# Reordering the first gathers, powers and weight loads of each layer in a four-layer perceiver kernel, with a shared part placed amid the causal tail

## The chip, the cores and the metric

One NeuronCore of a Trainium2 chip runs the whole kernel. The metric is device time in microseconds (us) of one execution; the median of three executions before the change is 2838.52 us (2836.55 to 2840.55).

The engines are named as the profile names them: PE (matrix products), PEld (weight loads of PE), DVE (vectors), ACT (activations), POOL (general purpose; it also issues the indirect gathers) and SP (issues most plain DMAs). Each engine runs its own instructions in one order and waits on semaphores for the others.

## The reference

The input x has 16 batches of 64 tokens with 256 features (1024 tokens); ctx has 16 x 1024 rows of 192. Four layers follow, each of three residual steps on the normalised x:

```python
# L0: cross attention to ctx, causal attention, mixture of 8 experts (top 2) with a shared expert
x = x + L0_xattn(layernorm(x), ctx, ctx); x = x + L0_attn(layernorm(x)); x = x + L0_ffn(layernorm(x))
# L1: cross attention (16 heads), convolution + running pooled attention + gelu layer, 8 experts top 2
x = x + L1_xattn(layernorm(x), ctx); x = x + L1_attn(layernorm(x)); x = x + L1_ffn(layernorm(x))
# L2: cross attention (8 heads of 64), complex linear recurrence, 8 experts top 2 with capacity
x = x + L2_xattn(layernorm(x), ctx); x = x + L2_attn(layernorm(x)); x = x + L2_ffn(layernorm(x))
# L3: cross attention (8 heads of 64), selective state space, dense layers with +1/-1 weights
x = x + L3_xattn(layernorm(x), ctx); x = x + L3_attn(layernorm(x)); x = x + L3_ffn(layernorm(x))
```

A mixture layer picks two experts per token by softmaxed logits, applies each expert's two- or three-matrix network, and adds the results weighted by the gates.

## The kernel before

All of x stays on chip as eight tiles `xs[:, i, :]` of 128 tokens by 256 features. The stages run one after another and overlap at their borders: `L0_first` (cross attention, causal attention and routing interleaved), `L0_ffn`, `L1_xattn`, `L1_attn`, `L1_ffn`, `L2_xattn_attn`, `L2_ffn` and `L3`.

**Who sets the order.** The kernel is written in a framework that places the instructions of each engine by a planner, in the order of the program and by when their inputs are ready. Inside `manual_schedule(engines=...)` the named engines keep the order of the program among the instructions written there; instructions written elsewhere may still be put between them. In most stages PE alone is fixed; at the start of `L1_xattn` (L1014) PE and DVE are. Python generators cut a job into pieces, and a stage calls `next` on them at chosen places so that one job's products fill another's waits.

**Mixture layers.** Routing (`route_setup` L1130 onwards, `route`, `block_experts` L1313) takes the logits, the two best experts, ranks the tokens of each expert, and sorts them into blocks of 128 tokens that have one expert each. `block_experts` yields after `rows` (which rows of the weight matrices a block gathers) and then makes `tokens` (which tokens it takes). A block gathers the weights `wa` and `wb` by `rows` and its tokens' features `hb` from the DRAM table `hs` by `tokens`, all on POOL through `gather_rows` (L1386), three buffers deep; it transposes hb on PE (L179), runs its products (`gu` or `ph`, then `po`), and writes `yb` to the DRAM table `ys` on ACT's queue (`block_out`, L1408 to L1410). `L0_ffn` has 23 blocks at most, the last 5 under a condition; `L1_ffn` 15. Padding reads a zero row of `hs` or `ys`, written by `zeros` (L1143); `route_setup` is called three times and writes the zero row of `hs` each time (L1140).

The next stage carries a tile (`carry`, L1388): two gathers `back` (or `p`) from `ys` by `route_at`, each added to xs by DVE (L1395). Then comes the normalisation: statistics on DVE (L154, L156, L158), a power on POOL (L160), and `o` on DVE (L458 in `heads64`, L890 in `L1_xattn`), which PE transposes.

**End of L0_first.** `attn.go()` is a round: each causal tile under way, and the routing of the group of two tiles that is at its turn, takes one step. After the last cross attention tile a loop calls `go` until nothing is left, and after each round one piece of the shared expert: `shared_part(k)` yields three times after a pair of gate and up products (`gu`, eight PE instructions) and twice after a down product (`po`, six). Chunk k is 256 tokens (tiles 2k and 2k+1). Chunks 0 and 1 go there; chunks 2 and 3 are written in `L0_ffn`, after both halves of `block_experts`, without a fixed order.

**Start of L1_xattn.** `keys_values(b)` gives four pieces (keys, values, keys, values) of PE work on a batch's context; their results leave the PSUM buffers `misc` through DVE or ACT. `queries(i)` carries and normalises tile i in its first step, transposes in its second, and makes qs with a copy by DMA in its third.

**L1_attn and L1_ffn.** The string `turns` (L1710) spells which of six generators steps next: parts 0 to 3 and the routing of tiles 0 to 3 and of tiles 4 to 7 (digits 2 and 5).

**L2_xattn_attn.** `recurrence()` (L1739) writes its set-up (powers on POOL L1749 and L1752, some 20 small DVE steps for angles from L1765 on, a sine on ACT) and returns the object whose `go` does a piece of the state recurrence. `heads64` does the cross attention and calls `breathe` (here `go`) at its filling places, first after tile 0 has been normalised.

**L3.** `first` multiplies two small matrices on PE (`large<-w_dt,w_xT`, 32 instructions). `weights` (L1988) issues the loads of L3a_in, L3a_bc and L3a_out, and through `fetch_L3_ffn` (L1910) those of the dense layers, on SP; some of them go as early as their room is free.

Of the kernel before, what the change touches and what calls it, by code (L numbers as in the profile page):

```python
# [42 lines left out]
class Net:  # L43
# [242 lines left out]
    def L0_first(self):  # L286
# [19 lines left out]
        with self.tc.manual_schedule(engines={mybir.EngineType.PE}):  # L306
# [90 lines left out]
            shared = chain(*(self.shared_part(k) for k in range(2)))  # L397
# [269 lines left out]
    def causal_attention(self, wqkv, wproj):  # L667
# [4 lines left out]
        s = SimpleNamespace(ready=0, next=0, work=[], behind=[])  # L672
# [138 lines left out]
        def routing(g):  # L811
# [41 lines left out]
    def L1_xattn(self):  # L853
# [160 lines left out]
        with self.tc.manual_schedule(engines={mybir.EngineType.PE, mybir.EngineType.DVE}):  # L1014
            biases()
            for piece, turn in zip(keys_values(0), (None, *[queries(0)] * 3)):
                piece()
                if turn is not None:
                    next(turn)
        with self.tc.manual_schedule(engines={mybir.EngineType.PE}):  # L1020
            held, work = None, {}
            one, two = queries(1), queries(2)
            ahead = (one,), (one, two), (one, two), (two,)
            steps = [(b, g) for b in range(B) for g in range(4)]
            for k in range(len(steps) + 4):
# [15 lines left out]
                if k < len(steps):  # L1041
                    if more:
                        more.pop(0)()
                    if not b:
                        for turn in ahead[g]:
                            next(turn)
                    elif b % 2 == 0 and g < 3 and b // 2 + 2 < NT:
                        if not g:
                            ahead = queries(b // 2 + 2)
                        next(ahead)  # L1050
# [76 lines left out]
    def route_setup(self, k):  # L1127
# [86 lines left out]
    def L0_block(self, j, own):  # L1214
        w = self.lp.tile([128, 4 * 704], F32, tag="wa" + own, bufs=1 if own else 3, name="wa")
        self.gather_rows(w, self.a["L0f_w13"], self.rows[j][:, j : j + 1])
        w2 = self.lp.tile([128, 6 * D], F32, tag="wb" + own, bufs=1 if own else 3, name="wb")
        self.gather_rows(w2, self.a["L0f_w2r"], self.rows[j][:, j : j + 1])
        return w.rearrange("p (c f) -> p c f", c=2), w2.rearrange("p (m f) -> p m f", f=D)
# [22 lines left out]
    def L0_ffn(self):  # L1242
        nc = self.nc
        self.blocks(self.routed, L0_BLOCKS)
        self.tag, self.tag_bufs = "gu", 4
        self.hid_tag, self.hid_bufs = "hid1", 3
        for k in range(2, NC):
            for _ in self.shared_part(k):
# [3 lines left out]
        def block(j, own=""):  # L1252
            w13, w2 = self.L0_block(j, own)
            dT = self.block_tokens(j, own)
# [50 lines left out]

    def blocks(self, r, n_blocks):


        rest = self.block_experts(r, n_blocks)
        next(rest)  # L1310
        next(rest, None)
# [87 lines left out]
    def block_tokens(self, j, own=""):  # L1399

        hb = self.lp.tile([128, D], F32, tag="hb" + own, bufs=1 if own else 3, name="hb")
        self.gather_rows(hb, self.hs, self.tokens[:, j : j + 1])
# [9 lines left out]
    def L1_block(self, j, own=""):  # L1412
        w = self.lp.tile([128, 2 * 1024 + 8], F32, tag="wa" + own, bufs=1 if own else 3, name="wa")
        self.gather_rows(w, self.a["L1f_W1b"], self.rows[j][:, j : j + 1])
        w2 = self.lp.tile([128, 8 * D], F32, tag="wb" + own, bufs=1 if own else 3, name="wb")
        self.gather_rows(w2, self.a["L1f_W2r"], self.rows[j][:, j : j + 1])
        return (
            w[:, : 2 * 1024].rearrange("p (c f) -> p c f", f=1024), w[:, 2 * 1024 :],
# [3 lines left out]
    def L1_ffn(self):  # L1422
        nc = self.nc
        def block(j, own=""):
            w1, b1, w2 = self.L1_block(j, own)
            dT = self.block_tokens(j, own)
# [106 lines left out]
    def L1_attn(self):  # L1533
# [970 lines left out]
```

## Time and profile before

| | |
|---|---|
| median of three executions | 2838.52 us |
| profiled execution, its own time | 2838.53 us |
| span of its trace | 2836.7 us |
| busy PE / PEld / DVE / ACT / POOL | 2603.1 / 1889.9 / 1399.4 / 1003.4 / 311.8 us |
| mean granted clock of PE | 0.963 |

The stretches about the places that the change touches, from the trace, with PE's busy time, the granted PE clock (1.00 is full) and the DMA engines' mean busy share:

| stretch, us from the start | what runs | PE busy, us | clock | DMA share |
|---|---|---|---|---|
| 60 to 255 | L0_first | 167.83 of 195 | 0.89 | 0.31 |
| 255 to 286 | causal tail, routing, first gathers of L0_ffn | 24.73 of 31 | 0.83 | 0.52 |
| 1083 to 1112 | end of L1_attn, first gathers of L1_ffn | 17.57 of 29 | 0.57 | 0.38 |
| 1220 to 1236 | start of L2_xattn_attn | 3.02 of 16 | 0.61 | 0.09 |
| 1930 to 1950 | start of L3 | 15.08 of 20 | 1.00 | 0.46 |

How to read it: the times are those of one profiled execution. A timeline line gives the start, the duration, the engine, the source line, the operation and its tiles (out<-in); the brackets at its end give the time the engine idled just before and what ended it. An instruction stands under the line of the helper that issued it: L69 is every product through `mm`, L62 and L64 are copies out of PSUM, L179 a transpose, L131 a weight load.

### The profile page before, as it was taken

To read this page: it belongs to the slowest core of one execution; us is meant where nothing else is said; L and a number is where in the kernel's file an instruction comes from. 1 tells how busy PE (TensorE), PEld (TensorE's weight loads), DVE (VectorE), ACT (ScalarE), POOL (GpSimd) and SP (SyncE) were. 2 spreads that over 40 slices of the span, in tenths; PEclk is the share of its full clock that TensorE was granted. 3 is DMA by queue.
4 is the path that set the end of the run, shared out by engine and by line. 5 is a ranking of instruction groups with operands and counts; after the bars stand their busy time and mean duration, and the time that the engine had idled before them with its cause. 6 is when DMAs were issued, how large, how long until landed. Compare 5 with 4: busy or idle time off the path is not lost.

```text
span 2836.7 us, 44734 instructions
## 1 busy us (share of the span) xinstructions
PE 2603.1 (92%) x18116; PEld 1889.9 (67%) x18116; DVE 1399.4 (49%) x2825; ACT 1003.4 (35%) x2114; POOL 311.8 (11%) x429
## 2 busy tenths in 40 slices
PE   7888998999999898979999999698999998998999
PEld 3556895666666686856666666695666665666777
DVE  3556225666666643233434342423344756658692
ACT  1323223555555441222222222122234545455330
POOL 1111333000000112310001000201001000000000
PEclk9988999999999997989999999799999999999999
DMA  8512872100100114801111111463112213121110
GB/s 244 174 49 77 339 271 65 31 27 28 38 27 23 42 38 176 305 25 47 59 58 55 45 49 59 181 239 108 51 49 91 86 49 97 56 76 30 61 45 8
DMA packets 79228, 253.71 MB, mean 89 GB/s; under 512 B 15151, under 2 KB 26954, under 8 KB 69290
## 3 DMA queue, kind: packets, MB, share of 16 engines
q1 hardware_dynamic: 59562, 165.01, 18.0%
q0 software_dynamic: 13312, 80.28, 7.9%
q10 hardware_dynamic: 6144, 5.51, 0.6%
q8 instruction: 145, 2.38, 0.3%
q14 instruction: 65, 0.53, 0.1%
HBM read 233.80 MB, written 14.82 MB: 88 GB/s over the span
## 4 chain that ended last, share of the span: by engine, by line
PE 38%; DVE 9%; ACT 3%; issue 2%; DMA 2%; POOL 1%; SPq 1%; DVEq 0%; ACTq 0%; POOLq 0%
PE sc L505 9%; PE ps_h L69 5%; PE misc L541 4%; PE halves L69 3%; PE misc L69 3%; PE ps_t L519 3%; PE halves L541 3%; PE misc L536 2%; PE gu L69 2%; DVE x L2104 2%; PE halves L2128 2%; PE halves L536 1%; DVE nmx L223 1%; DVE x L2100 1%; DMA rep<-dus 1%
## 5 line engine op out<-in xcount | busy, mean ns | idle before, releaser
L223 DVE TENSOR_REDUCE nmx<-sc 128x1 f32<-128x1024 f32 x264 | 311.7, 1218 | 228.4 <-PE sc L505 144.8
L225 ACT ACTIVATE p<-sc,nmx 128x1024 f32<-128x1024 f32 x264 | 294.2, 1115 | 313.5 <-DVE nmx L223 313.3
L505 PE MATMUL sc<-ctxT,qp 128*128 128x512 f32 (+1 forms) x1024 | 357.5, 603 | 0.0
L505 PEld LDWEIGHTS sc<-ctxT,qp 128*128 128x128 f32 (+1 forms) x1024 | 139.4, 190 | 155.4 <-issue 152.3
L519 PE MATMUL ps_t<-ident,p 128*128 128x128 f32 x1024 | 140.2, 279 | 40.2 <-ACT pT L522 17.3
L2094 ACT ACTIVATE da<-rep,al 128x252 f32<-128x252 f32 x256 | 115.9, 500 | 134.4 <-DVE x L2104 124.2
L519 PEld LDWEIGHTS ps_t<-ident,p 128*128 128x128 f32 x1024 | 115.3, 142 | 65.2 <-ACT pT L522 21.0
L2104 DVE TENSOR_TENSOR_SCAN x<-da,x 128x512 f32<-128x512 f32 x128 | 152.7, 1218 | 2.7 <-ACT da L2094 1.9
L235 PE MATMUL misc<-ident,p 128*128 128x128 f32 x1024 | 137.1, 279 | 7.2 <-ACT p L225 6.8
L522 ACT COPY pT<-ps_t 128x512 f32<-128x512 f32 x166 | 94.0, 587 | 122.0 <-PE ps_t L519 116.1
L235 PEld LDWEIGHTS misc<-ident,p 128*128 128x128 f32 x1024 | 110.1, 141 | 32.7 <-ACT p L225 15.4
L160 POOL TENSOR_TENSOR ln_rs<-ln_ve,nhalf 128x1 f32<-128x1 f32 x80 | 44.9, 567 | 692.8 <-DVE ln_ve L158 611.0
L541 PE MATMUL halves<-pT,ctx 128*128 128x256 f32 x512 | 119.3, 386 | 0.0
L541 PE MATMUL misc<-pT,ctx 128*128 128x256 f32 x512 | 119.1, 386 | 0.0
L237 ACT COPY pT<-misc 128x512 f32<-128x512 f32 x128 | 75.0, 586 | 108.6 <-PE misc L235 108.1
L69 PE MATMUL ps_h<-r,w 128*128 128x256 f32 x512 | 113.4, 381 | 0.0
L2100 DVE TENSOR_TENSOR x<-rep,bc_rep 128x512 f32<-128x512 f32 x128 | 84.7, 687 | 57.9 <-PE halves L2128 55.2
L239 DVE COPY pT<-misc 128x512 f32<-128x512 f32 x128 | 88.3, 690 | 39.7 <-PE misc L235 28.6
L69 PEld LDWEIGHTS ps_h<-r,w 128*128 128x128 f32 x512 | 96.6, 190 | 15.9 <-issue 2.5
L541 PEld LDWEIGHTS halves<-pT,ctx 128*128 128x128 f32 x512 | 94.8, 190 | 17.3 <-issue 5.6
L541 PEld LDWEIGHTS misc<-pT,ctx 128*128 128x128 f32 x512 | 94.6, 190 | 17.1 <-issue 5.5
L69 PE MATMUL po<-wb,hid 128*128 128x256 f32 x440 | 100.3, 379 | 0.0
(500 smaller groups left out, 4504.3 us busy)
## 6 DMA issues: line engine op xcount, KB each, us to landing
ctx<-in_ctx SPq DMA_DIRECT2D x48, 768.0 KB, 4.4
ctxT<-in_ctxT SPq DMA_DIRECT2D x48, 512.0 KB, 3.3
w<-in_L2f_W SPq DMA_DIRECT2D x24, 1024.0 KB, 8.3
rep<-dus SPq DMA_DIRECT2D x256, 64.0 KB, 1.9
ctxT<-in_ctxT SPq DMA_DIRECT2D x16, 768.0 KB, 15.5
ctxT<-in_ctxT SPq DMA_DIRECT2D x96, 128.0 KB, 3.5
ys<-yb ACTq DMA_DIRECT2D x40, 128.0 KB, 5.7
bc_rep<-bcs SPq DMA_DIRECT2D x32, 128.0 KB, 3.0
```

Of the source, the lines that this page charges most:

```text
L69: self.nc.tensor.matmul(out, lhsT, rhs, start=n == 0, stop=n == len(pairs) - 1)
L223: self.nc.vector.tensor_reduce(nmx, sc, AX.X, ALU.max, negate=True)
L225: self.nc.scalar.activation(p, sc, AF.Exp, bias=nmx, accum_out=sums)
L235: self.nc.tensor.transpose(ps[:, u, :], p[:, at : at + 128], self.ident)
L239: self.nc.vector.tensor_copy(pT[:, 0:4, :], ps)
L505: nc.tensor.matmul(sc[u][:, bass.ts(kh, 512)], qp[n][par][rows, h : h + 2, :].rearrange("p h q -> p (h q)"), ctx[0][rows, at], start=n == ...
L519: nc.tensor.transpose(ps[:, t, :], p[:, at : at + 128], self.ident)
L522: nc.scalar.copy(to, ps)
L541: nc.tensor.matmul(o, ck[:, t, :128], pT[:, t].rearrange("p u q -> p (u q)"), start=t == 0, stop=t == NK - 1)
L2094: nc.scalar.activation(da[:, g, :, 1:], now[j][:, 0, :].rearrange("p (b s) -> p b s", s=S)[:, :, 1:], AF.Exp, scale=al[:, col : col + 1],)
L2100: nc.vector.tensor_tensor(h, now[j][:, 1:2, :].to_broadcast([128, 2, CHUNK]), bc[:, 0, states, :], ALU.mult)
L2104: nc.vector.tensor_tensor_scan(flat, da.rearrange("p g b s -> p (g b s)"), flat, 0.0, ALU.mult, ALU.add)
```

## The change

There are six edits.

1. `zeros` copies from the last row of the causal mask tile, which is zero throughout, in 4 packets of 256 bytes in place of 256 packets of 4; the zero row of `hs` is written by the first routing only.
2. Chunk 2 of the shared expert joins the loop at the end of `L0_first`. A part begins only when the features of its tiles are there (`turned`, set in the routing generator). In `L0_ffn`, PE is now fixed: first half of `block_experts`, two pieces of chunk 3, second half, the rest of chunk 3.
3. At the start of `L1_xattn` POOL is fixed too, and six pieces of keys and values (four of batch 0, two of batch 1) alternate with three steps of tile 0's queries.
4. The second routing of `L1_attn` yields after two of its four tiles' logits, and `turns` gives it one step earlier.
5. The first block of `L0_ffn` and of `L1_ffn` gathers wa, hb, wb in that order, fixed on POOL (before: wa, wb, hb); the other blocks as before.
6. At layer 2 `recurrence()` is made at the first call of `breathe`; at layer 3 six one-column copies of the updated tile 0 go into the rooms of the weights before their loads are issued.

```diff
             del self.ctxT[2:], self.ctx[2:]
-            shared = chain(*(self.shared_part(k) for k in range(2)))
+
+            def parts():
+                for k in range(3):
+                    while attn.turned <= k:
+                        yield
+                    yield from self.shared_part(k)
+
+            shared = parts()
             while attn.go():
                 next(shared, None)
...
+            s.turned = g + 1
             ps = self.misc([128, 2, E])
...
-        with self.tc.manual_schedule(engines={mybir.EngineType.PE, mybir.EngineType.DVE}):
+        with self.tc.manual_schedule(
+            engines={mybir.EngineType.PE, mybir.EngineType.DVE, mybir.EngineType.Pool}
+        ):
             biases()
-            for piece, turn in zip(keys_values(0), (None, *[queries(0)] * 3)):
-                piece()
-                if turn is not None:
+            turn = queries(0)
+            ahead = keys_values(0) + keys_values(1)
+            for n in range(6):
+                ahead.pop(0)()
+                if n in (1, 3, 4):
                     next(turn)
...
-                        more = keys_values(b + 1) if b + 1 < B else None
-                    if not k:
-                        more.pop(0)()
+                        more = ahead if not b else keys_values(b + 1) if b + 1 < B else None
...
-        self.zeros(self.hs[:1])
+        if self.routed is None:
+            self.zeros(self.hs[:1])
...
     def zeros(self, row):
         self.nc.sync.dma_start(
-            row.rearrange("p (d o) -> p d o", o=1), self.lanes[:1, :1].unsqueeze(1).to_broadcast([1, D, 1])
+            row.rearrange("p (r d) -> p r d", d=S), self.causal[S - 1 : S].unsqueeze(1).to_broadcast([1, D // S, S])
         )
...
+    def gathered(self, j, own, first, second):
+
+        got = []
+        with self.tc.manual_schedule(engines={mybir.EngineType.Pool}) if not j else nullcontext():
+            order = ("wa", "hb", "wb") if not j else ("wa", "wb", "hb")
+            for name in order:
...
     def L0_ffn(self):
         nc = self.nc
-        self.blocks(self.routed, L0_BLOCKS)
         self.tag, self.tag_bufs = "gu", 4
         self.hid_tag, self.hid_bufs = "hid1", 3
-        for k in range(2, NC):
-            for _ in self.shared_part(k):
+        with self.tc.manual_schedule(engines={mybir.EngineType.PE}):
+            experts, part = self.block_experts(self.routed, L0_BLOCKS), self.shared_part(NC - 1)
+            next(experts)
+            for _ in range(2):
+                next(part)
+            next(experts, None)
+            for _ in part:
                 pass
...
         def routing(first):
             ps = self.misc([128, 4, E])
             for t in range(4):
+                if first and t == 2:
+                    yield
...
-        turns = "0010130134013004314101340301301403101341041134031434234323424242455555"
+        turns = "00101301340130043141013403013014031013410411340314342343234242452455555"
...
         with self.tc.manual_schedule(engines={mybir.EngineType.PE}):
-            lru = self.recurrence()
-            self.heads64(breathe=lru.go, finished=lru.more)
+            made = []
+
+            def lru():
+                if not made:
+                    made.append(self.recurrence())
+                return made[0]
+
+            self.heads64(breathe=lambda place: lru().go(place), finished=lambda i: lru().more(i))
...
         def weights():
-            for n, to in zip(("in", "bc", "out"), (w[0], w[2], w[3])):
+            rooms = w[0], w[2], w[3], self.spent[0], w[4], self.spent[1]
+            for to in rooms:
+                nc.vector.tensor_copy(to[:, 0, :1], self.xs[:, 0, :1])
+            for n, to in zip(("in", "bc", "out"), rooms):
                 nc.sync.dma_start(to, self.a[f"L3a_{n}"])
             yield
-            self.ffn = self.fetch_L3_ffn((self.spent[0], w[4], self.spent[1]))
+            self.ffn = self.fetch_L3_ffn(rooms[3:])
```

More of the change, by code (lines that the diff above doesn't have):

```diff
@@ L671, in causal_attention @@
         nc = self.nc
-        s = SimpleNamespace(ready=0, next=0, work=[], behind=[])
+        s = SimpleNamespace(ready=0, next=0, turned=0, work=[], behind=[])
         sb = self.sb
@@ L1022, in L1_xattn @@
             one, two = queries(1), queries(2)
-            ahead = (one,), (one, two), (one, two), (two,)
+            turns = (one,), (one, two), (one, two), (two,)
             steps = [(b, g) for b in range(B) for g in range(4)]
@@ L1044, in L1_xattn @@
                     if not b:
-                        for turn in ahead[g]:
+                        for turn in turns[g]:
                             next(turn)
@@ L1048, in L1_xattn @@
                         if not g:
-                            ahead = queries(b // 2 + 2)
-                        next(ahead)
+                            turn = queries(b // 2 + 2)
+                        next(turn)
                 if held is not None:
@@ L1212, in route, with L0_block @@
             self.over_experts(g, ALU.add, "", r.gates[x][:, tiles])
[L1214 to L1219, printed above, removed]
+    def gathered(self, j, own, first, second):
[3 more added lines that the diff above has]
+            for name in order:
+                bufs = 1 if own else 3
+                if name == "hb":
+                    hb = self.lp.tile([128, D], F32, tag="hb" + own, bufs=bufs, name="hb")
+                    self.gather_rows(hb, self.hs, self.tokens[:, j : j + 1])
+                else:
+                    src, n = first if name == "wa" else second
+                    w = self.lp.tile([128, n], F32, tag=name + own, bufs=bufs, name=name)
+                    self.gather_rows(w, self.a[src], self.rows[j][:, j : j + 1])
+                    got.append(w)
+        return hb, *got
+    def L0_block(self, j, own=""):
+        hb, w, w2 = self.gathered(j, own, ("L0f_w13", 4 * 704), ("L0f_w2r", 6 * D))
+        return hb, w.rearrange("p (c f) -> p c f", c=2), w2.rearrange("p (m f) -> p m f", f=D)
     def shared_part(self, k):
@@ L1252, in block @@
         def block(j, own=""):
-            w13, w2 = self.L0_block(j, own)
-            dT = self.block_tokens(j, own)
+            hb, w13, w2 = self.L0_block(j, own)
+            dT = self.block_tokens(hb)
             hid = self.lp.tile([128, 6, 128], F32, tag="hid1", bufs=3, name="hid1")
@@ L1304, in ranks @@
         return rank
[L1306 to L1311, printed above, removed]
     def block_experts(self, r, n_blocks, later=False):
@@ L1397, in carry, with block_tokens @@
             )
-    def block_tokens(self, j, own=""):
-        hb = self.lp.tile([128, D], F32, tag="hb" + own, bufs=1 if own else 3, name="hb")
-        self.gather_rows(hb, self.hs, self.tokens[:, j : j + 1])
+    def block_tokens(self, hb):
         dT = self.lp.tile([128, 2, 128], F32, tag="dT", bufs=2, name="dT")
@@ L1412, in L1_block @@
     def L1_block(self, j, own=""):
[L1413 to L1416, printed above, removed]
+        hb, w, w2 = self.gathered(j, own, ("L1f_W1b", 2 * 1024 + 8), ("L1f_W2r", 8 * D))
         return (
-            w[:, : 2 * 1024].rearrange("p (c f) -> p c f", f=1024), w[:, 2 * 1024 :],
+            hb, w[:, : 2 * 1024].rearrange("p (c f) -> p c f", f=1024), w[:, 2 * 1024 :],
             w2.rearrange("p (m f) -> p m f", f=D),
@@ L1424, in block @@
         def block(j, own=""):
-            w1, b1, w2 = self.L1_block(j, own)
-            dT = self.block_tokens(j, own)
+            hb, w1, b1, w2 = self.L1_block(j, own)
+            dT = self.block_tokens(hb)
             hid = self.lp.tile([128, 8, 128], F32, tag="hid", bufs=2, name="hid")
@@ L1732, in L2_xattn_attn @@
         with self.tc.manual_schedule(engines={mybir.EngineType.PE}):
-            lru = self.recurrence()
-            self.heads64(breathe=lru.go, finished=lru.more)
+            made = []
[4 more added lines that the diff above has]
+            self.heads64(breathe=lambda place: lru().go(place), finished=lambda i: lru().more(i))
             self.start_pack(self.at)
-            while lru.go():
+            while lru().go():
                 pass
```

## The prediction

> **What bounds the kernel now.** I read the page's first two blocks first. Its busy times, and the slices of PE and of its granted clock:
>
> ```profile
> PE 2603.1 (92%) x18116; PEld 1889.9 (67%) x18116; DVE 1399.4 (49%) x2825; ACT 1003.4 (35%) x2114; POOL 311.8 (11%) x429
> ...
> PE   7888998999999898979999999698999998998999
> ...
> PEclk9988999999999997989999999799999999999999
> ```
>
> PE is busy for 92% of 2836.7 us, so the time is PE's work plus PE's waits. The dips stand where a layer begins, and there the clock falls too. Next I read PE's timeline at each start that the diff touches: end of layer 0's causal attention, layer 1's cross attention, layer 1's experts, layer 2 and layer 3. Columns are start, duration, engine, line, operation, and in brackets the idle time with what ended it.
>
> ```profile
> 255.77 1.03 PE L69 MATMUL misc<-w,yT 128*128 128x256 f32 x4
> ...
> 260.78 4.13 PE L69 MATMUL gu<-hT,w 128*128 128x256 f32 x18
> ...
> 268.29 1.94 PE L69 MATMUL misc<-s_col,s_who 128*64 128x128 f32 x8 [2.83 <-DVE s_col L1186]
> 270.17 0.60 PE L69 MATMUL misc<-route_seen,ones 128*128 128x8 f32 x2
> 273.01 4.64 PE L69 MATMUL gu<-hT,w 128*128 128x256 f32 x10 [2.25 <-DVE hid L1234]
> 277.58 0.57 PE L69 MATMUL misc<-at_block,route_table 64*128 64x23 f32 x2
> 278.08 2.87 PE L69 MATMUL misc<-w,hid 128*128 128x256 f32 x12
> ...
> 284.67 0.38 PE L179 MATMUL misc<-ident,hb 128*128 128x128 f32 x2
> ```
>
> ```profile
> 454.77 0.66 PE L179 MATMUL misc<-ident,o 128*128 128x128 f32 x2 [4.68 <-DVE o L890]
> ...
> 467.07 1.13 PE L69 MATMUL sc<-kT,qs 32*128 32x512 f32 x4 [2.21 <-DMA qs<-qs]
> ```
>
> ```profile
> 1110.41 0.69 PE L179 MATMUL misc<-ident,hb 128*128 128x128 f32 x2 [2.10 <-DMA hb<-hs,tokens]
> ```
>
> ```profile
> 1232.95 0.66 PE L179 MATMUL misc<-ident,o 128*128 128x128 f32 x2 [12.47 <-DVE ln_mv L156]
> ```
>
> ```profile
> 1931.26 13.90 PE L69 MATMUL large<-w_dt,w_xT 128*128 128x512 f32 x32
> 1949.39 0.44 PE L179 MATMUL halves<-ident,o 128*128 128x128 f32 x2 [4.24 <-DVE o L458]
> 1950.39 3.65 PE L69 MATMUL large<-hT,w 128*128 128x128 f32 x16 [0.56 <-issue]
> ```
>
> In the first fence shared-expert products (gu) fill nearly every wait of layer 0's tail, so the chain from projection 255.77 to block counts 270.17 costs PE little. The others show true waits of 4.68, 2.21, 2.10, 12.47 and 4.24 us. Only these, and the time that a late chain adds, can change.
>
> **Part 1: the zero row.** Before, 256 packets of 4 bytes, three times; after, 4 of 256 bytes, once. Such a packet takes 9 ns in the trace: 256 x 9 / 16 engines = 0.14 us of DMA. The issue takes SP 0.59 us against 0.33 for a plain load. Only the first issue (18.91 us) is near busy DMAs. I take **-0.2** (0 to -1).
>
> **Part 2: the shared part in the causal tail.** Parts 0 and 1 already go one piece per round. A part is three gu pieces of 1.99 us and two po pieces of 1.47: 8.9 us. After the change part 2's pieces go in rounds 11 to 15, in PE's fixed order ahead of the last tile's weighing and projection; the planner had put only 1.13 us (gu, 254.80) there. So the projection comes 8.9 - 1.13 = 7.8 us later; I take 7.7. Projection to end of counts is a chain of small DVE steps, 15.0 us now. It ends at 270.77 + 7.7 = 278.5. The 4.13 us of gu that hid inside it (260.78) are gone from there, so PE idles in it. Part 3 is then fixed behind the counts: 24 gu and 12 po instructions, 8.9 us at full clock; at the half clock, by the rows 273.01 (4.64/10 = 0.464 each) and 278.08 (2.87/12 = 0.239 each), 11.1 + 2.9 = 14.0. I take the middle, 11.5, with 0.57 for the tokens: PE reaches block 0 at 290.6 instead of 284.67. Its tokens agree: two pieces (16 gu at a mean of 0.36, 5.7) and the product 0.57 end at 284.8; from there to the gathered rows took 283.48 - 278.15 = 5.3 us, so 290.1. Weights: the gather issued at 274.40 landed at 281.01, so 7.7 later 288.7, hidden by part 3. That the second weights now gather behind hb costs 0.95 us of POOL issue, needed only after 44 products (5.15 us). Term **+5.9**. Bounds: 0, if the chain waits for DVE anyway and the pieces lie in that wait; above, 14.0 for part 3 (293.1, +8.4) and block 0's 5.15 at half clock too: +13.6.
>
> The granted clock in the profile is 0.50 from 267.72 to 277.96, after PE's 2.83 us wait, and 0.97 from 264 to 268. The Trainium skill, TensorE: Matmul & The Clock Gate, section Part 1: The HAM clock gate, says that the array falls to half rate after an idle window of about 3.4 us and comes back after one sustained busy window; it speaks against moving work out of waits, as here. By it only part 3's first 3.4 us would be slow, 1.7 us more than 8.9, and the term +5.0; the row's 10.24 us is three such windows, so I stay with the rows.
>
> **Part 3: layer 1's cross attention.** PE waits 4.68 us for o of tile 1 (L890). Its adds end at 450.9, its variance at 452.16, but POOL issues two gathers for other tiles (451.19, 452.44) before the power at 453.54. POOL's fixed order puts the power ahead of them: up to 1.4 us. DVE's order holds kT's eviction (454.55) behind that o, and the next keys' products need the bank: so the wait can't be filled altogether. One key or value piece (2.9 us) of batch 1 goes ahead of scores, in place of a later one; it can cover the 2.21 us wait for qs, whose copy took 4.2 us beside a context load. I take 1.4 + about 0.3: **-1.7** (bounds -5, from 4.68 + 2.21 less their 2.9 us of filler missing later, and +1, a POOL gather of 0.95 queued behind a power that waits).
>
> **Part 4: layer 1's routing and first block.** Four tiles' logits take PE 1086.28 to 1091.57. Two go a turn earlier, so the chain starts about 1.4 us sooner. Behind it, hb is gathered before the second weights: issued 1104.14 before, landed 1110.37. Together hb lands near 1106.5 and the 2.10 us wait goes; PE's gate work before it ends 1.4 sooner, 1107. But DMA runs full from 1102 to 1128, and block 1's rows (landed 1117.68, used 1119.95) become late next: about 2.2 us of slack. I take **-1.2** (0 to -3).
>
> **Part 5: layer 2's start.** ys lands at 1223.72; POOL gathers at once, then runs a power of the recurrence's set-up (1224.70, 0.89), gather 2 (1226.87) and another power (1227.91, 0.59). DVE stands at L1792 behind that power until 1228.5, so the carry's add, whose rows landed at 1226.50, runs at 1229.99 only. Made after the first two tiles, the set-up can't stand there: the add runs at 1226.6, 3.4 sooner; PE at 1229.5. Up to 3.85 if the gather's landing alone decides. About 21 DVE steps of 0.15 to 0.25 us and a table load of 1.28 come later, beside score products of 7.25 us. I take **-3.3** (-1 to -3.85).
>
> **Part 6: layer 3's weights.** About 3.3 MB of loads are issued on SP before the last block's rows are written:
>
> ```profile
> 1930.28 0.33 SPq L1990 DMA_DIRECT2D w<-in_L3a_in  x1
> ...
> 1931.60 0.58 SPq L1910 DMA_DIRECT2D w<-in_L3f_k  x1
> ```
>
> The write issued at 1931.64 by ACT landed 8.25 us later, with a DMA share of 0.95 and 0.82 in the two stretches of 4 us from 1932; the same write at layer 2's start took 2.68 (1221.04 to 1223.72). The four gathers went at 1941.09 and after. Six one-column copies of DVE, which read the updated tile 0, hold the loads back. The gathers then go some 5.6 to 6.3 us sooner. PE has w_dt x w_xT until 1945.16, so it gains the idle 4.24 and, the clock (granted 0.50 from 1950.49 to 1953.91) no longer falling, most of 3.65 - 1.95 (the same 16 products at 1982.03) = 1.7: **-5.9** (-3, half of the write's delay being other than these loads, to -7.5). The copies cost 6 x 0.15 us of DVE; SP has no issue between 1931.60 and 1974.54, so nothing queues behind the held loads, which then run while DMA is nearly idle (1948 to 1972). Without this cover, their 2.7 MB would take 8 us of the context loads. The weights are first read near 2060.
>
> **Sum:** -0.2 + 5.9 - 1.7 - 1.2 - 3.3 - 5.9 = -6.4. The profiled execution took 2838.53 us (span 2836.7 and 1.8 around it), the median 2838.52, so it carries over: **2832.1 us**. About 0.2% (5.7 us) is what a measurement can tell from no change: below 2832.8 counts as faster, above 2844.2 as slower.
>
> **Rivals.**
> *The tail decides (slower).* Part 2 at its full price: the chain pushed 7.7 and the clock half over part 3 and block 0, +13.6. For it: 10.24 us at half clock after an idle time of only 2.83; against it: gu pieces warm the array. It overtakes the five gains (12.3) from +12.3. With them whole the time is 2839.8; with layers 2 and 3 at their small ends (-1, -3) it is 2845.
> *Larger gain.* The pieces lie in the tail's DVE waits (part 2 at +1), and both waits of layer 1's attention go (-4): -0.2 + 1 - 4 - 2 - 3.5 - 6.5 = -15.2, 2823. For it: PE waited in that stretch often enough for 3.6 us of filler; against it: kT's bank.
> *It doesn't do what it says.* The write of ys is slow for another reason than these loads, and layer 2's add waits for its landing: -0.2 + 5.9 - 1 - 0.5 - 1 - 3 = +0.2, 2838.7. For it: the last write always ends after a block of big loads; against it: 2.68 us at layer 2.
>
> **Chances.** Forecast 0.42 (own range 2828 to 2836; 0.25 of it below 2832.8), larger gain 0.22, not as said 0.20 (all within), tail 0.16 (0.13 above 2844.2, 0.03 within). Faster 0.47, same 0.40, slower 0.13. The range runs from 2822 to 2845: the larger gain and the tail's dear end just in.
>
> **What would show it.** The counts' product near 278 and block 0's rows near 290; the wait before o of tile 1 nearer 3 than 5; hb's wait gone at layer 1's experts; layer 2's first product near 1229 less the shift; the last write in 3 us at layer 3 and no idle time before its first transposes. It would be wrong if the counts come at their old distance, or if the first gathers at layer 3 aren't sooner.

## The result and the profile after

The changed kernel took 2848.01 us (median of 9 runs, 2844.14 to 2852.86) against 2838.52 (2834.1 to 2844.97): a ratio of 1.0033, 95% interval 1.0022 to 1.0045. It is 9.5 us slower, where the forecast was 2832.1 and faster. The profiled execution has a span of 2846.2 us, 9.5 more than before.

From the page of the changed kernel:

```profile
PE 2608.7 (92%) x18116; PEld 1892.2 (66%) x18116; DVE 1402.5 (49%) x2831; ACT 1003.2 (35%) x2114; POOL 310.1 (11%) x429
```

PE does the same 18116 products; its busy time has grown by 5.6 us (the same products, part of them at a lower clock) and its waits by 3.9.

A good way to find where two executions of one program part is to match each product with its twin and to follow how far the later one lags. The lag (after minus before, in us) is -0.4 at 40, -9.5 at 56, -10.9 at 200 to 240, -2.8 at the block counts, -4.1 at block 0 of layer 0, +1.4 from block 2 on; +2.4 in layer 1's attention, +8.6 at the end of its experts, +9.9 in layer 2; +10.1 at the end of layer 2, +5.0 at the start of layer 3, +9.4 at the end. So there is an early gain that the forecast hadn't, a loss of 12.3 us between 240 and 300, the expected gain at layer 3, and several small losses. Every lag in this document is taken against one profile of the kernel before; how far that profile itself is from other executions is told below.

PE's timeline of the changed kernel at the places shown before, first the end of the causal tail:

```profile
267.36 0.60 PE L69 MATMUL misc<-route_seen,ones 128*128 128x8 f32 x2
269.53 6.04 PE L69 MATMUL gu<-hT,w 128*128 128x256 f32 x16 [1.58 <-DVE past L1352]
275.50 0.40 PE L69 MATMUL misc<-at_block,route_table 64*128 64x23 f32 x2
...
280.58 0.38 PE L179 MATMUL misc<-ident,hb 128*128 128x128 f32 x2
...
293.08 0.44 PE L179 MATMUL misc<-ident,hb 128*128 128x128 f32 x2 [3.71 <-DMA hb<-hs,tokens]
```

Counts 8.1 us and block 0 6.8 us later against the stretch before them (lag -10.9), near the 7.7 and 5.9 worked out; most of the two pieces of chunk 3 ahead of the tokens runs at half clock (6.04 us for 16 products; the granted clock is 0.50 from 257.22 to 274.28). New is the last line: block 1 waits 3.71 us for its rows.

Then layer 1's cross attention, layer 1's experts, layer 2, layer 3 on PE, and layer 3's loads on SP:

```profile
458.03 0.44 PE L179 MATMUL misc<-ident,o 128*128 128x128 f32 x2 [2.00 <-DVE ln_ve L158]
...
468.27 3.26 PE L948 MATMUL misc<-w,ctxT 128*128 128x256 f32 x8 [4.28 <-DVE kT L939]
```

```profile
1115.53 0.69 PE L179 MATMUL misc<-ident,hb 128*128 128x128 f32 x2
...
1126.76 0.44 PE L179 MATMUL misc<-ident,hb 128*128 128x128 f32 x2 [0.84 <-DMA hb<-hs,tokens]
```

```profile
1242.44 0.66 PE L179 MATMUL misc<-ident,o 128*128 128x128 f32 x2 [13.34 <-DVE ang_y L1792]
```

```profile
1955.08 0.38 PE L179 MATMUL halves<-ident,o 128*128 128x128 f32 x2
1956.02 2.02 PE L69 MATMUL large<-hT,w 128*128 128x128 f32 x16 [0.56 <-ACT w L2011]
```

```profile
1953.69 0.33 SPq L2018 DMA_DIRECT2D w<-in_L3a_in  x1
```

In layer 1 one wait has been exchanged for another twice (4.68 + 2.21 for 2.00 + 4.28; 2.10 for 0.84 one block later). Layer 2 waits 0.9 us longer than before. Layer 3 is as forecast: no wait, and the 16 products in 2.02 in place of 3.65.

The early gain stands in PE's waits for the second context load. Before:

```profile
45.94 1.94 PE L340 MATMUL sc<-ctxT,qp 96*64 96x512 f32 x2 [3.81 <-DMA ctxT<-in_ctxT]
49.68 6.82 PE L340 MATMUL sc<-ctxT,qp 96*64 96x512 f32 x14 [1.79 <-DMA ctxT<-in_ctxT]
```

After:

```profile
43.38 3.65 PE L340 MATMUL sc<-ctxT,qp 96*64 96x512 f32 x14 [0.78 <-DMA ctxT<-in_ctxT]
```

The first wait is gone, the second is 0.78 us, and the 14 products take 3.65 us at full clock (granted 1.00 from 18.28 to 72.90; before 0.50 from 45.86 to 56.10). A wait of 1.47 us for the same tensor comes later, at 56.67. In before, the packets of 4 KB of that load, issued at 34.63, took up to 5.97 us each, in the 7 us after 256 packets of 4 bytes had been written, most of them from 32 to 33.

### The profile page after: what moved, and what is told of

Same layout as the page of the kernel before. It is cut to its first block, busy times and chain, and to the rows that moved or that the text cites. A ratio compares the mean times of both kernels' runs of the same rounds, so it can differ in the third digit from the quotient of the medians.

```text
span 2846.2 us, 44754 instructions
## 1 busy us (share of the span) xinstructions
PE 2608.7 (92%) x18116; PEld 1892.2 (66%) x18116; DVE 1402.5 (49%) x2831; ACT 1003.2 (35%) x2114; POOL 310.1 (11%) x429
## 4 chain that ended last, share of the span: by engine, by line
PE 40%; DVE 9%; ACT 3%; issue 2%; DMA 2%; POOL 1%; SPq 1%; ACTq 0%; DVEq 0%; POOLq 0%
PE sc L512 9%; PE ps_h L69 5%; PE misc L548 4%; PE halves L69 3%; PE misc L69 3%; PE ps_t L526 3%; PE halves L548 2%; PE gu L69 2%; PE misc L543 2%; PE halves L2156 2%; DVE x L2132 2%; DVE nmx L223 1%; PE halves L543 1%; PE po L69 1%; PE large L69 1%
## 5 line engine op out<-in xcount | busy, mean ns | idle before, releaser
L235 PEld LDWEIGHTS misc<-ident,p 128*128 128x128 f32 x1024 | 110.0, 141 | 34.2 <-ACT p L225 16.7
```

Source lines behind the costliest of these rows:

```text
L235: self.nc.tensor.transpose(ps[:, u, :], p[:, at : at + 128], self.ident)
```

## The experiments

Each kernel was timed in 6 to 12 runs beside the kernel before; ratios are to it, and 0.001 is 2.84 us. The median of before differed from one comparison to the next (2839.4, 2841.0, 2842.2, 2843.0 us), so medians are compared only inside one. The first theory was read off the two traces: the zero row brings 8 us, the tail costs 7, the order of the first gathers costs 6, layer 3 brings 5. The rival was the prediction's own list of prices.

### Four kernels for the four large terms

**Zero rows alone** (before with both hunks of edit 1):

```diff
-            row.rearrange("p (d o) -> p d o", o=1), self.lanes[:1, :1].unsqueeze(1).to_broadcast([1, D, 1])
+            row.rearrange("p (r d) -> p r d", d=S), self.causal[S - 1 : S].unsqueeze(1).to_broadcast([1, D // S, S])
```

> Before with the first edit alone: the zero rows in 4 packets of 256 bytes, that of hs written once. Theory (traces of before and after): the 256 packets of 4 bytes hold up the reads that come right after them; in before, the context load issued at 34.63 us has packets of 4 KB that took up to 5.97 us, PE waits 3.81 and 1.79 us for ctxT and the clock falls, and in after these waits are 0 and 0.78. So 8 us less than before (6 to 11): about 2830. Rival (the prediction's first term): only the packets' own 0.14 us and the issue count, -0.2: 2838.

Measured: 0.9988 (0.9976 to 0.9999), -3.3 us. The trace's first wait for ctxT is gone, the second is 0.72, and its lag is -7.8 us at the end. The sign is the theory's, the timed size (interval 0.3 to 6.8 us) is less than half of it.

**The changed kernel with the old gather order:**

```diff
-        with self.tc.manual_schedule(engines={mybir.EngineType.Pool}) if not j else nullcontext():
-            order = ("wa", "hb", "wb") if not j else ("wa", "wb", "hb")
+            order = ("wa", "wb", "hb")
```

> The changed kernel with block 0's gathers in the old order (wa, wb, hb), in both mixture layers. Theory: the second weights held behind hb leave the DMA engines idle (share 0.61, 0.53, 0.81 in three stretches of 4 us from 272 us), and block 1's rows then come late (PE waits 3.71 us at 293.08 and the clock falls), and in the same way 1 to 3 us in layer 1. So 6 us less than the changed kernel (4 to 9): about 2842, and no wait ahead of block 1 in layer 0. Rival: block 1 is late because the whole tail came late against the block's fixed transfer time: then the order changes nothing, or gives back the 2.10 us wait at layer 1: 2848 to 2850.

Measured: 1.0008 (0.9998 to 1.0018), that is 7 us less than the changed kernel's 1.0033. The wait ahead of block 1 is gone:

```profile
291.78 0.44 PE L179 MATMUL misc<-ident,hb 128*128 128x128 f32 x2
```

The second and third windows of 4 us after the first gather's issue show why; columns are stretch, PE, PEld, DVE, ACT and POOL busy (instructions), clock, DMA share, GB/s. Changed kernel:

```profile
275.31:279.31 4.00, 3.94 (x19) 3.00 (x18) 0.93 (x3) 0.77 (x2) 2.12 (x3) 1.00 0.63 250
279.31:283.31 4.00, 3.37 (x24) 2.92 (x23) 1.18 (x3) 0.00 (x0) 3.15 (x5) 1.00 0.81 264
```

The same with the old order:

```profile
277.60:281.60 4.00, 3.94 (x18) 3.06 (x18) 0.93 (x3) 0.77 (x2) 2.12 (x3) 1.00 0.99 403
281.60:285.60 4.00, 3.34 (x22) 2.62 (x21) 1.27 (x3) 0.00 (x0) 3.21 (x5) 1.00 0.97 350
```

All engines do about the same, only the DMA engines stand idle more while wb, held behind hb, isn't issued: wb goes at 278.06, 6.75 us after wa, against 1.53 us with the old order. In this stretch, which the DMA engines fill, bytes not moved at once made block 1 late. On POOL of the changed kernel:

```profile
276.80 0.95 POOL L1408 DMA_INDIRECT hb<-hs,tokens  x1 [4.28 <-DVE tokens L1374]
278.06 0.94 POOL L1408 DMA_INDIRECT wb<-in_L0f_w2r,rows  x1 [0.30 <-issue]
```

**The changed kernel with the old tail** (edit 2 undone):

```diff
-            shared = parts()
+            shared = chain(*(self.shared_part(k) for k in range(2)))
...
-            for _ in range(2):
-                next(part)
-            next(experts, None)
-            for _ in part:
-                pass
+        next(experts, None)
+        for k in range(2, NC):
+            for _ in self.shared_part(k):
+                pass
```

> The changed kernel with the second edit undone: two parts in the causal tail, two parts without a fixed order behind the block plan. Theory: the counts come 8 us after their place in the changed order less the filler given back, so block 0 starts 6 to 7 us sooner and the stretch after it is bound by the gathers: 5 to 7 us less than the changed kernel, 2841 to 2843. Rival (the tail costs nothing, its pieces lie in waits): 2848 within 2.

Measured: 0.9997 (0.9984 to 1.0010), 10 us less than the changed kernel, more than the 5 to 7 expected. Block 1's wait is 1.37 us here, not 3.71: part of what the order costs goes with the tail.

**Layer 3's copies alone** (before with the last two hunks of the change):

```diff
+            rooms = w[0], w[2], w[3], self.spent[0], w[4], self.spent[1]
+            for to in rooms:
+                nc.vector.tensor_copy(to[:, 0, :1], self.xs[:, 0, :1])
```

> Before with the copies at layer 3 alone, which hold the weight loads back until tile 0 is carried. Theory (as predicted, -5.9; the traces' offset between the kernels falls from 10.09 to 3.86 to 4.96 us there): 5 us less than before, 2833 to 2834. Rival: the held loads or the changed phase of the clock give it back in the state space (the offset grows by 4.4 us from 2100 us on in the trace): 2838 within 2.

Measured: 0.9986 (0.9977 to 0.9995), -4.0 us. In the trace the lag falls by 6.1 us up to 1955, of which 5.0 are left at 1975 and 3.4 at the end. So the expectation's rival has a part in it: some of the gain is given back in the state space.

### Each loss by itself, and a repair

**The tail alone** (before with edit 2):

```diff
-            shared = chain(*(self.shared_part(k) for k in range(2)))
+            shared = parts()
...
+            experts, part = self.block_experts(self.routed, L0_BLOCKS), self.shared_part(NC - 1)
```

> Before with the second edit alone: chunk 2 of the shared expert in the causal tail, chunk 3 fixed between the two halves of the block plan; gathers in the old order. Theory: the counts come 7 to 8 us later and block 0 about 7 us later (the traces of the changed kernel give 6.8, with the old gathers 6.9); block 1 isn't late beyond that, because the old order keeps the DMA engines busy while PE does chunk 3: 2839.4 + 7 = 2846. Rival (the tail alone makes block 1 late as well, as in the changed kernel): +12, 2851.

Measured: 1.0027 (1.0013 to 1.0041), +7.7 us. Counts 7.2 and block 0 6.3 us later (7.0 and 6.1 against the lag of 0.2 ahead of them); block 1 waits 0.19.

**The gather order alone** (before with edit 5):

```diff
+        with self.tc.manual_schedule(engines={mybir.EngineType.Pool}) if not j else nullcontext():
+            order = ("wa", "hb", "wb") if not j else ("wa", "wb", "hb")
```

> Before with the order wa, hb, wb of block 0 alone, in both mixture layers, fixed on POOL. Theory: with the old tail the tokens come 4 us after the rows, so the second weights are held only about 3 us and block 1 is late by 1 to 2 us in layer 0; in layer 1 the gain of the 2.10 us wait is given back by the next blocks: together +1.5, 2839 to 2842. Rival 1 (the order alone costs the 5.7 us that undoing it in the changed kernel gave): 2845. Rival 2 (prediction: -1.2 or so at layer 1): 2838.

Measured: 1.0008 (0.9994 to 1.0021), +2.3 us, unclear by itself. Block 1 waits 0.72 us in layer 0; in layer 1 the 2.10 us are gone, and 0.59 and 0.82 stand at later blocks.

**The zero row twice** (the write of 256 packets of 4 bytes issued once more; it writes the same zeros):

```diff
-        self.zeros(self.hs[:1])
+        for _ in range(2 if self.routed is None else 1):
+            self.zeros(self.hs[:1])
```

> Before with the first zero row written twice, in 256 packets of 4 bytes each time (the output is the same). Theory (each such write holds up the reads behind it): the context load right behind waits longer, 3 us or more on top of before, 2842 to 2847, and in the trace the two waits for ctxT near 45 us (3.81 and 1.79) grow. Rival (the waits come from something else in that stretch): 2839, waits as before.

Measured: 1.0017 (1.0005 to 1.0029), +4.8 us. The second wait for ctxT is 6.57 us in place of 1.79:

```profile
54.54 6.85 PE L340 MATMUL sc<-ctxT,qp 96*64 96x512 f32 x14 [6.57 <-DMA ctxT<-in_ctxT]
```

**A repair of layer 2's start.** Zero rows and layer 3's copies, and a recurrence whose base vector reads tile 1 after that tile's last update, so that the set-up can't come first:

```diff
-        nc.vector.memset(e1, float(np.e))
+        nc.vector.tensor_scalar(e1, self.xs[:, 1, :3], 0.0, float(np.e), ALU.mult, ALU.add)
```

> Before with the zero rows, the copies at layer 3 and a recurrence made late whose base vector is computed from tile 1 (times 0, plus e), so that no step of the set-up can stand ahead of the first two tiles. Theory: the two other edits bring -3 and -4, and PE's first product of layer 2 comes about 3.5 us sooner after ys has landed (9.2 us before, 10.1 in the changed kernel, where DVE still did the set-up first): 2839.4 - 11 = 2828.5. Rival (the set-up, moved, holds up the tiles that follow): 2832 and a new wait of 3 us near 1240.

Measured: 0.9962 (0.9946 to 0.9977), 10.8 us less than before, and the fastest kernel of the study. But little of that is layer 2's. Its first transposes come 8.2 us after the first gather's issue (9.2 before), and then the rival's wait stands in PE's timeline:

```profile
1224.25 0.66 PE L179 MATMUL misc<-ident,o 128*128 128x128 f32 x2 [11.47 <-DVE ln_ve L158]
...
1232.07 1.16 PE L69 MATMUL misc<-qT,w 64*128 64x128 f32 x16 [2.86 <-DVE qT L470]
```

qT waits behind the set-up's small steps on DVE, 2.86 us in place of 0.78. Over the stage the lag falls by some 0.7 us.

### The small edits alone, and them together with the gains

**The start of layer 1's cross attention alone** (edit 3):

```diff
+            engines={mybir.EngineType.PE, mybir.EngineType.DVE, mybir.EngineType.Pool}
...
+            ahead = keys_values(0) + keys_values(1)
+            for n in range(6):
+                ahead.pop(0)()
+                if n in (1, 3, 4):
                     next(turn)
```

> Before with the third edit alone (start of layer 1's cross attention). Theory from the traces: the waits of 4.7 (o) and 2.0 us (qs) give way to 1.8 (o) and 4.2 us (the eviction of kT, which DVE's fixed order holds behind other steps), so the sum of PE's waits stays within 1 us: 2839 to 2841, same as before. Rival (prediction): -1.7, with the wait for qs gone and nothing in its place.

Measured: 1.0004 (0.9995 to 1.0014). PE's timeline:

```profile
452.63 0.44 PE L179 MATMUL misc<-ident,o 128*128 128x128 f32 x2 [1.80 <-DVE ln_ve L158]
...
457.42 1.16 PE L69 MATMUL misc<-hT,w 128*128 128x128 f32 x8 [1.58 <-DVE v L62]
462.89 3.35 PE L942 MATMUL misc<-w,ctxT 128*128 128x256 f32 x7 [4.32 <-DVE kT L933]
```

1.80 + 1.58 + 4.32 = 7.7 us of waits where before had 4.68 + 2.21 = 6.9. That is as the theory has it: no gain, within 1 us.

**The routing in two steps alone** (edit 4):

```diff
+                if first and t == 2:
+                    yield
...
-        turns = "0010130134013004314101340301301403101341041134031434234323424242455555"
+        turns = "00101301340130043141013403013014031013410411340314342343234242452455555"
```

> Before with the fourth edit alone (second routing of layer 1 in two steps, one of them earlier). Theory from the trace of the changed kernel: the two early tiles' logits push the products with gT, then the last tiles' chain; the counts come 1 us later, not sooner: 2840 to 2842. Rival (prediction): the chain starts 1.4 us sooner, 2838.

Measured: 1.0001 (0.9990 to 1.0013). From the last tiles' transposes to block 0's rows it takes 23.7 us, against 24.7. But the transposes themselves come later: the two early tiles' logits stand on PE ahead of the products with gT, and the lag, -4.35 ahead of them, is -2.99 at those products and at the transposes and -4.03 at the block counts. So the counts come 0.3 us later, not 1.4 sooner; that is the theory's sign, with less than its 1 us, and the prediction's mechanism isn't seen. Block 0's 32 products then take 6.51 us, part of them at half clock, against 5.09.

**The late recurrence alone:**

```diff
-            lru = self.recurrence()
+            def lru():
+                if not made:
+                    made.append(self.recurrence())
+                return made[0]
```

> Before with the recurrence made late alone, as in the changed kernel. Theory: DVE isn't in a fixed order there, its set-up steps are still placed ahead of the carry's adds, and POOL's powers now stand behind the second gather: PE's first product of layer 2 comes about 10 us after the gather of tile 0 is issued, against 9.2 before: +1, 2840 to 2842. Rival (prediction): -3.3, 2836.

Measured: 1.0008 (0.9996 to 1.0020); PE waits 13.35 us ahead of the first transposes, against 12.47. As the theory has it, though the time alone doesn't settle it.

**The repaired kernel with edit 3:** the hunks of edits 1, 3 and 6 and the repair:

```diff
-        nc.vector.memset(e1, float(np.e))
+        nc.vector.tensor_scalar(e1, self.xs[:, 1, :3], 0.0, float(np.e), ALU.mult, ALU.add)
...
+            ahead = keys_values(0) + keys_values(1)
```

> Zero rows, copies at layer 3, the third edit, and the recurrence made late with its base computed from tile 1; the tail, the turns and the gathers as before. Theory: as the same kernel without the third edit (0.9962 of before) within 1 us: 2829 to 2831. Rival (the third edit is worth its 1.7 after all): 2828.

Measured: 0.9982 (0.9969 to 0.9996). Faster than before; it doesn't beat the one without edit 3 (0.9962), and the two intervals overlap, so edit 3's worth stays within what these runs can tell.

### Is the whole dearer than its parts?

Alone, the edits come to -1.2 (zero) + 2.7 (tail) + 0.4 + 0.1 + 0.8 (order) + 0.8 - 1.4 (layer 3) = +2.2 thousandths; the change costs 3.3. Each part is known to about 1 thousandth and the sum of the seven therefore to about 3, so the times alone don't tell the two apart. The traces do, in one place. From 240 to 320 us the lag grows by 12.3 us in the changed kernel, by 6.4 with the tail alone and by 1.1 with the order alone; in the nine kernels that have neither it grows by 0.0 to 0.9. Those are single profiles, but variants of the changed kernel agree: 7.0 and 6.4 with the old order of gathers (in both layers, in layer 0), 1.6 with the old tail. Four more kernels were run on that and on the size of the zero row.

**Tail and order together, without the rest:**

```diff
+            shared = parts()
...
+            order = ("wa", "hb", "wb") if not j else ("wa", "wb", "hb")
```

> Before with the second and the fifth edit (tail and order of the first gathers). Theory: the two make each other dearer, since the held weights now wait for tokens that stand behind two pieces of chunk 3: +13 (7.7 of the tail and 5.4 of block 1's wait and the clock after it), 2853 to 2855, and PE waits 3 to 4 us ahead of block 1. Rival (they add up): +10, 2850 to 2852, and PE waits 1 us there.

Measured: 1.0050 (1.0033 to 1.0066), +14.2 us (9.4 to 18.8); alone they had 7.7 and 2.3, and by these times the two could still add up. In the trace the lag grows by 12.4 us from 240 to 320, as in the changed kernel, against 6.4 + 1.1 alone: together they cost 4.9 us more. The wait ahead of block 1 lies between the sum and the expected 3 to 4:

```profile
299.70 0.44 PE L179 MATMUL misc<-ident,hb 128*128 128x128 f32 x2 [2.19 <-DMA hb<-hs,tokens]
```

**The changed kernel with the token product straight behind the counts:**

```diff
             next(experts)
-            for _ in range(2):
-                next(part)
             next(experts, None)
             for _ in part:
```

> The changed kernel with the token product directly behind the counts, ahead of all of chunk 3. Theory: hb and with it the second weights are issued 3 to 4 us sooner after the first weights, the DMA engines idle less, and block 1's wait of 3.71 us falls to 1 or less: 4 us less than the changed kernel, 2844. Rival (block 1 is late for the tail's sake): 2848 and a wait of 3 to 4 us as before.

Measured: 0.9997 (0.9985 to 1.0009), 10 us less than the changed kernel by the ratios, more than the 4 expected. Now hb goes 1.53 and wb 2.79 us after wa, and block 1 doesn't wait:

```profile
273.61 0.62 PE L69 MATMUL misc<-at_block,route_table 64*128 64x23 f32 x2 [3.72 <-DVE at_block L1368]
274.16 8.41 PE L69 MATMUL gu<-hT,w 128*128 128x256 f32 x24
...
294.30 0.38 PE L179 MATMUL misc<-ident,hb 128*128 128x128 f32 x2
```

So the two edits are tied by one step: wb waits for hb, hb for the tokens, the tokens stand on PE behind 16 products of chunk 3, most of them at half clock. It isn't free: PE now waits 3.72 us for the token product's input and all of chunk 3's gu products come behind it (8.41 us for 24). From 240 to 320 the lag grows by 8.9 us instead of 12.3, so 3.4 us are gained there, near the expectation; the rest of the 10 isn't seen in this stage.

**The old order in layer 0 only:**

```diff
-            order = ("wa", "hb", "wb") if not j else ("wa", "wb", "hb")
+            order = ("wa", "hb", "wb") if not j and second[1] == 8 * D else ("wa", "wb", "hb")
```

> The changed kernel with the old order of block 0's gathers in layer 0 only; layer 1 keeps wa, hb, wb. Theory: the whole 5.7 us that the old order gave in both layers comes from layer 0; in layer 1 the 2.10 us wait that goes is made up by waits of the next blocks: 2842 to 2843. Rival (layer 1's order is worth its 2 us): 2840.

Measured: 0.9996 (0.9984 to 1.0008), against 1.0008 (0.9998 to 1.0018) with the old order in both. All of the loss that the order brings is layer 0's (from 240 to 320 the lag grows by 6.4 us, as with the tail alone); for layer 1 nothing can be told.

**The zero row four times:**

```diff
-        self.zeros(self.hs[:1])
+        for _ in range(4 if self.routed is None else 1):
+            self.zeros(self.hs[:1])
```

> Before with the first zero row written four times, 256 packets of 4 bytes each (the output is the same). Theory: each write more holds the following reads up by the 4 to 5 us that the second one cost (zero_twice: +4.8 timed, the second wait for ctxT 6.57 in place of 1.79): 12 to 15 us over before, 2852 to 2855. Rival (only the first ones matter, or the packets' own 0.14 us): within 6.

Measured: 1.0085 (1.0067 to 1.0104), +24 us, 8 for each further row, well over the 4 to 5 expected. PE's waits:

```profile
52.98 6.10 PE L340 MATMUL sc<-ctxT,qp 96*64 96x512 f32 x14 [6.76 <-DMA ctxT<-in_ctxT]
...
80.47 1.97 PE L340 MATMUL sc<-ctxT,qp 96*64 96x512 f32 x2 [14.36 <-DMA ctxT<-in_ctxT]
```

Packets of 6 KB whose read began in the 6 us from 54.0 and from 65.5, behind the third and the fourth burst, have a median of 2.0 us and go up to 7.1 and 6.9, against 0.23 to 0.24 at most other times. That the cost lies in the reads behind the writes, and not in the writes' own packets (7 to 9 ns), is shown; the mechanism in the memory isn't, nor whether the size of the packets or their number to one row does it.

## Why the prediction was wrong

**The step that failed** is in part 2: "That the second weights now gather behind hb costs 0.95 us of POOL issue, needed only after 44 products (5.15 us)." It asked when block 0 needs wb, and not what the DMA engines do meanwhile. They were the bound from 278 to 306 (share 1.02 in before); for layer 1 the working did ask that question, and made block 1 late there. Holding wb for 6.75 us left them idle for about 2.1 us more than the old order does (shares of 0.63 and 0.81 against 0.99 and 0.97 in two windows of 4 us), and block 1's wait of 3.71 and the slow clock behind it (0.50 from 294.76 to 298.18) followed: the old order in the changed kernel is 7 us faster.

**Part 2's other half was right.** Counts +7.7 forecast, 7.2 measured alone; block 0 +5.9 forecast, 6.3 measured; the time +7.7. The rival with the tail in it had the right place and sign, with the wrong carrier: not the clock through part 3 and block 0 (in the changed kernel part 3 with the token product took 11.2 us, and block 0's 44 products 5.18, at full clock), but block 1's rows. One row was misread: 278.08 (2.87 for 12) lies behind the half-clock stretch, which ends at 277.96, so 14.0 is not part 3 at half clock throughout, and the rival's price was put too low. Nothing of the result rests on it.

**Part 1** was right in sign and far too small: -0.2 (0 to -1), against -3.3 timed alone, and 4.8 (written twice) to 8 (four times) for each further row. The working priced the packets and not what stands behind them; the trace of before showed it, in the 3.81 us wait for a load issued 11 us sooner and in a share of 0.74 at only 45 GB/s from 34 to 40 us. The Trainium skill, DMA: Bandwidth & Descriptors, Specifications, says that transfers under 512 bytes are read, modified and written and miss the line rate; that fits a bad price for 4-byte packets, but not its place, which here is the reads after them. By the same page (Latency and other measured facts) an access to the memory takes 2 us under high load; 5.97 us for a packet of 4 KB is well above that, though no run here shows an access by itself.

**Part 3**: -1.7 forecast, nothing measured (1.0004). kT's bank, which the working named as the bound, took the wait over in full: in the changed kernel DVE did seven adds of other tiles' carries first, with a wait of 1.33 us for one gather among them, before it evicted kT. The lower bound of -5 isn't the sum it names, either: 4.68 + 2.21 less 2.9 is 4.0.

**Part 4**: the 1.4 us of the logits weren't gained: alone, the counts come 0.3 us later, because the logits that go early stand ahead of the products with gT and of the last tiles' transposes on PE. The wait of 2.10 us for hb does go with the new order, and it made the next blocks late, as feared (0.84 in the changed kernel, 0.59 and 0.82 alone).

**Part 5**: -3.3 forecast; alone the wait grows by 0.9 us and the time by 2.3 (-1.1 to 5.7). "Made after the first two tiles, the set-up can't stand there" is false: program order isn't DVE's order where DVE isn't fixed. In the changed kernel DVE still stands at the set-up, waits there for POOL's power, does the angle, and only then the carry's add:

```profile
1237.27 0.15 DVE L1776 TENSOR_SCALAR neg<-ex 128x1 f32<-128x1 f32 x1 [9.38 <-POOL ex L1774]
...
1239.12 0.26 DVE L1806 TENSOR_SCALAR ang<-lanes,phi_y 128x64 f32<-128x64 f32 x1
1239.29 0.48 DVE L1417 SCALAR_TENSOR_TENSOR xs<-p,route_g,xs 128x256 f32<-128x256 f32 x1
```

Only a dependence on data moved it, and then the work that was moved showed up as a wait one step later.

**Part 6** was right in its mechanism: -5.9 (-3 to -7.5) forecast, -4.0 timed (interval -1.4 to -6.5), 5 to 6 in the trace at layer 3's start: the last write of ys landed 1.7 us after its issue, not 8.25. (The loads are 2.7 MB, as its later sentence has it, not 3.3.) The timed value is smaller, and the trace says where: in the state space from 2100 on the lag grows by 1.0 to 4.4 us in the eight profiles with the held loads, and by -0.3 to 1.9 in the nine without. Whether the loads or the phase of the clock bring that isn't shown.

The sum was wrong by 16 us: about 8 from the tail with the held gather (5.9 forecast, 14.2 timed and 12.4 in the trace for the two together), some 10 from parts 3 to 5 (-6.2 forecast, +3.7 as the sum of the three alone, each unclear by itself), 2 from layer 3, less the 3 that the zero row gave beyond its forecast.

**Why the zero row's trace shows 8 us and the timed runs 3.3** is in part settled by the other traces. At 56 us the eight kernels with the new rows are 8.0 to 9.8 us ahead of before's profile, and the seven others that write the old row once are between 0.9 ahead and 1.1 behind: the gain is 9 us there. At 200 us the first are 8.8 ahead on average (5.8 to 11.5) and the second already 3.3 (from 7.9 ahead to 1.1 behind), though they change nothing up to there. So before's profile is a slow one in that stretch, and the edit is worth some 6 us at 200, inside the timed interval of 0.3 to 6.8.

In the same way, from 320 to 1925 five kernels that leave layers 1 and 2 as they were, but for zero rows, lose 2.5 to 7.2 us on before's profile (mean 4.6), and five with all of parts 3 to 5, or all but an order of gathers, lose 4.7 to 9.2 (mean 7.0). The small edits therefore cost about 2 us together, instead of the 6.2 gained by the forecast. How they share it stays open; it lies inside the runs' spread.

## What to carry to other kernels

Where the DMA engines bound a stretch, as they did here, ask of an order of transfers first whether it leaves them idle; putting a transfer back behind one that can't be issued yet cost more here than the wait it removed. A late tile and a held gather cost more together than apart (12.4 us in the trace against 6.4 + 1.1), so edits on one chain should be tried singly and in pairs. A chain's length says little when its start has moved: take the lag at both ends. And one profile of the kernel before is a poor yardstick for a few us; the other kernels that leave a stretch alone show how much it moves by itself. An order that only the program states is no order for an engine that a planner fills: state it by data or fix that engine.

## What the runs showed of the hardware

A row of zeros written by 256 packets of 4 bytes slows the reads that come in the next 6 us or so: the median packet of 6 KB took 2.0 us in place of 0.23, while the written packets themselves take 7 to 9 ns each, and the row costs the kernel 3.3 to 8 us. And PE's granted clock is 0.50 or 1.00 in these traces, nearly always in stretches of 3.41 us or a multiple of it (6.83, 10.24, 13.65). In nine kernels that don't touch layer 3, the stretch from 2100 to the end took from 0.3 us less to 1.9 more than in before; in the changed kernel it took 4.4 more, with 34.2 us at half clock between 2100 and 2650 in place of 23.9. The first 200 us moved by up to 7.9 in kernels that leave them alone. A gain under 2 us has to be read off its own stage.
